# A four-layer graph-attention kernel: x ahead of the other loads at the start, its second part issued from ACT's queue, and a new set of due times

## The chip, the cores and the metric

The kernel runs on one core of one Trainium2 chip. The metric is the device time of one execution in microseconds (us); the median of six runs is given, and one further execution was taken with the hardware profiler. The core's engines each run their own instruction stream in order: TensorE (PE, with its weight loads as PEld), VectorE (DVE), ScalarE (ACT), GpSimd (POOL) and SyncE (SP), which issues most DMAs. They wait for one another by semaphores.

## The reference

x has 16 graphs of 1024 nodes and 256 features in float32; adj is one symmetric 1024 x 1024 adjacency matrix for all. Four attention layers follow each other. Each takes h = relu(layernorm(x)) and adds to x:

```
layer 0, 3:  Wh = h W (4 heads of 64); e_ij = leaky(s_i + t_j) per head, from two score vectors a
             softmax over j where adj_ij is set; out = elu(alpha Wh)
layer 1:     the same with one head of 256
layer 2:     e_ij = leaky((h W1)_i . (h W2)_j); out = relu(softmax(e) (h W3))
x = x + out
```

## The kernel before, in words

`tile_gnn_stack` runs `fast`, and a general version only where a check of the inputs fails; it does not run here. A "batch" is one graph, a unit of work is (batch, layer), and 64 of them are interleaved.

In layers 0, 1 and 3 the exponential of a leaky score is written as a maximum of products of per-node factors, so that no score matrix is computed: DVE makes a 128 x 512 tile p = max(row, ke) * mask in one instruction (`weigh`, line 1117 for the four-head layers 0 and 3, line 1208 for layer 1), and PE multiplies it with val (`attend`, into the accumulators acc, or accb for layers 1 and 2). A four-head unit has 64 such p tiles. A pool of 8 p buffers lies between DVE and PE. In layer 2 PE computes the scores (`score`), ACT takes exponentials (lines 1235 and 1236) and DVE finishes them (1240, 1241). `product` (line 579) issues every matmul of this kind as two of 64 columns, at line 582.

A unit begins with its prologue: `statistics` (lines 822, 823, on DVE, one pair for each 128 nodes), `norm`, `norm2`, `norm3` (rstd on DVE line 855, the power on POOL line 858, nshift on DVE line 861), h on ACT (line 891), a transposition of h, the projection by w on PE, and its eviction on ACT (lines 972, 975) and, in some units, DVE (line 983). The transposition goes through planes (ACT line 914), a DMA transpose issued by SP (line 918) and a copy (ACT line 932), but for the first unit (0, 0) and the last (15, 3), where `direct` is set: there PE transposes (lines 906, 929), the work is cut in parts of 2, 2 and 4 tiles (`PARTS`) or 4 and 4, and the factor rows come from PE (`spread`, lines 1025, 1029) and not over DRAM (lines 1051, 1064). A unit ends with reciprocal (1150), division (1161, 1164), elu (1083 to 1097; the sum with x on POOL at line 1097 where `filling` is set, else DVE line 1090) and, after layer 3, a store (1188).

The x tiles, one per batch, have five buffers; at the start four of them hold raw quarters of adj. `load_x` (line 628) loads a batch in parts. `weight` (line 645) loads a weight matrix and its score vectors, and puts their products into extra columns (line 684 the products, 697 or 701 the sums); for w0, loaded from ACT's queue, all of this runs on DVE, for the others the products are on POOL. `mask_steps` (line 721) loads the quarters of adj on SP (729), compares them on DVE (737), transposes on PE (595) and keeps them as bytes (750).

None of this is written in the order in which it runs. Each piece is added to a `Plan` (line 79) with an engine, an assumed cost, a due time, what it comes after, and what buffers it takes and gives. `Plan.order` (line 102) walks through assumed time: an idle engine takes, of the pieces that are ready and whose buffers are free, the one with the smallest due time. The resulting list is the order of the instructions. An "after" only shapes this list; the waits on the chip come from the data. The due times come from tables at the top (lines 49 to 73): START, LEAD, STEP, WHEN and EARLY for all units in periods of 190, LATER and AHEAD for single units of batches 0 to 3 and 12 to 15. So a changed cost or due time near the start can move work in all of the run.

Of the kernel before, what the change touches and what calls it, by code (L numbers as in the profile page):

```python
# [43 lines left out]
PARTS = (((0, 4), (4, 8)), ((0, 2), (2, 4), (4, 8)))  # L44

PERIOD, EARLY = 190.0, 0.7407
START = {0: 0.0, 1: 1.0372, 2: 2.297, 3: 3.5524}  # L50
LEAD = {0: 0.7046, 1: 0.4612, 2: 0.2956, 3: 1.6786}
STEP = {0: 0.01, 1: 0.0686, 2: 0.0892, 3: 0.0445}
WHEN = {
    (1, "weights"): ((-0.5242, 0.0026), (-0.1464, 0.0419)),
    (1, "attended"): ((0.7567, 0.0147), (0.2574, 0.106)),
    (2, "weights"): ((-0.0331, 0.0103), (0.3531, 0.0135)),
    (2, "attended"): ((0.642, 0.0926), (0.4636, 0.0079)),
}

LATER = {  # L60
    (1, 0): 0.596, (1, 1): 0.958, (13, 2): 0.03, (13, 3): 0.392, (14, 3): -0.089, (0, 2): -0.137, (12, 2): 0.2,
    (13, 1): -0.61, (13, 0): 0.042, (0, 1): 0.165, (14, 2): 0.012, (12, 3): 0.381, (15, 2): 0.061,
    (14, 1): 0.153, (0, 3): -0.204, (0, 0): 0.005, (15, 1): 0.169, (3, 0): -0.106, (3, 2): -0.226,
    (3, 1): -0.037, (3, 3): 0.253, (14, 0): -0.403, (15, 3): 0.422, (12, 0): 0.216, (2, 2): -0.002,
    (2, 3): -0.052, (12, 1): -0.053, (1, 3): 0.022,
}
AHEAD = {
    (1, 0): 0.818, (15, 3): 0.338, (12, 1): 1.914, (15, 1): 0.404, (1, 3): -1.162, (0, 3): 0.168,
    (14, 2): 0.163, (14, 1): -0.3, (1, 1): -0.058, (0, 2): 0.142, (13, 1): 0.271, (3, 1): 0.197, (14, 3): 0.426,
    (3, 3): -0.404, (2, 2): 1.115, (15, 0): -0.042, (12, 0): 0.12, (1, 2): 0.321, (2, 3): -0.168,  # L70
    (3, 2): -0.354, (2, 1): -0.221, (13, 3): -0.364, (0, 1): 0.057, (12, 3): 0.014, (0, 0): -0.016,
    (13, 2): -0.254,
}
# [466 lines left out]
def fast(  # L540
# [87 lines left out]
    def load_x(b, due, after=()):  # L628

        res = []  # L630
        for t0, t1 in PARTS[b == 0]:

            def fn(its=slice(t0, t1)):
                if its.start == 0:
                    x_tiles[b] = buf("x", [P, NT, F], name="xt")
                nc.sync.dma_start(
                    out=x_tiles[b][:, its, :], in_=x[b].rearrange("(t p) f -> p t f", p=P)[:, its, :]
                )

            s = plan.add(SP, 0.5, due, fn, after, take=() if t0 else ("x",))  # L640
            after = (s,)
            res += [landed(s, due, 128 * (t1 - t0))] * (t1 - t0)
        return res

    def weight(w, name, due, a=None, heads=0, own=1):
# [9 lines left out]

        s = landed(plan.add(engine, 0.5, due, load), due, 256)
        if a is None:
# [10 lines left out]

        s2 = landed(plan.add(engine, 0.5, due, load_a, take=("p1",)), due, own * d)

# [7 lines left out]
        for c in range(KC):  # L678

            def columns(c=c):  # L680
                wa = tiles["wa", c] = buf("u", [P, heads, 2, d], name="wa")
                for side in range(2):
                    of = tiles["a"][:, :, side, :]
                    (nc.vector if first else nc.gpsimd).tensor_mul(
                        wa[:, :, side, :],
                        t[:, c, :F].rearrange("p (h d) -> p h d", h=heads),
                        of if own == heads else of.to_broadcast([P, heads, d]),
                    )

            m = plan.add(*((DVE, 0.7) if first else (POOL, 2.0)), due + 0.5, columns, (s, s2, *done), take=("u",))  # L690
            done = []
            for hd in range(1 if first else heads):

                def add_up(c=c, hd=hd):
                    wa, to = tiles["wa", c], t[:, c, F:].rearrange("p (s h) -> p h s", s=2)
                    if first:
                        nc.vector.tensor_reduce(to, wa, AX.X, OP.add)
                        return
                    for side in range(2):
                        junk = small.tile([P, F], BF16, name="junk_a", bufs=1)[:, :d]  # L700
                        nc.scalar.activation(
                            junk, wa[:, hd, side, :], AF.Identity, accum_out=to[:, hd, side : side + 1]
                        )

                give = () if not first and hd < heads - 1 else ("u", "p1") if c == KC - 1 else ("u",)
                done.append(
                    plan.add(*((DVE, 0.6) if first else (ACT, 1.1)), due + 0.5, add_up, (m, *done[-1:]), give=give)
                )
        return t, done[-1]

    first_x = load_x(0, SOON)

# [3 lines left out]

    w0, w0_ready = weight(w_l0, "w0", SOON, a_l0, 4, 4)
    plan.add(ACT, 1.6, SOON, warm)
    plan.add(DVE, 0.2, SOON, lambda: nc.vector.tensor_copy(ident_b, ident))

    def mask_steps():
        done = {}
        for n, (half, jh) in enumerate(((0, 0), (0, 1), (1, 0), (1, 1))):
            due, quarter = 15.0 + n if half else SOON + n, {}

# [4 lines left out]

            loaded = landed(plan.add(SP, 0.9, due, load, take=("x",)), due, 1024)
            for t in range(HT):
# [5 lines left out]

                s = plan.add(DVE, 0.45, due, positive, (loaded,), take=("h",), give=("x",) if t == HT - 1 else ())

# [10 lines left out]

                s = plan.add(*((ACT, 0.6) if half else (DVE, 0.45)), due, keep, (s,), give=("pp",))
                done.setdefault((half, jh), []).append(s)
# [11 lines left out]
    def w12_steps(due):  # L765
        tiles, last = {}, []
        for k, w in enumerate((w1_l2, w2_l2)):
# [4 lines left out]

            loaded = landed(plan.add(SP, 0.5, due, load, take=("p1",)), due, 256)
            for cc in range(KC):
# [53 lines left out]
    class Layer:  # L828
# [7 lines left out]
        def prologue(self, due, step, stats, direct=False):  # L836
# [12 lines left out]
            for n, its in enumerate(slice(*part) for part in parts):  # L849
# [28 lines left out]

                at = due - (len(parts) - n - 1)
                s = plan.add(DVE, 0.2, at, norm, (*stats[its], ready[-1] if n else None))  # L880
                s = plan.add(POOL, 2.0, at, norm2, (s,))
                take = () if n else (tag,) if self.gat else (tag, "hq")
                ready += [plan.add(DVE, 0.2, at, norm3, (s,), take=take)] * (its.stop - its.start)
            copies, evicted = [], []
            for n, t0 in enumerate(range(0, NT, 2)):
# [37 lines left out]
                def kept(t0=t0):  # L923
                    if self.gat:
                        T["hT", t0] = buf("hTp", [P, KC, 2 * P])
                    else:
                        T["hT", t0] = self.hT[:, :, t0 * P : (t0 + 2) * P]
                    if direct:
                        nc.scalar.copy(T["hT", t0], T["tp", t0])
                        return  # L930
                    bits = T["hT", t0].bitcast(U16).rearrange("p c (q s) -> p c q s", s=2)
                    nc.scalar.copy(bits, T["tp", t0].rearrange("p s c q -> p c q s"))  # L932

                take = ("hTp",) if self.gat else ()
                if direct:
                    s = plan.add(PE, 0.47, at, turned, (s,), take=("pp",), give=("h", "h"), wide=True)
# [8 lines left out]
                for k in range(2):  # L945
# [40 lines left out]
                    cost = 0.32 if many or not self.gat else 0.65 if heads == 1 else 1.05  # L986
                    s2 = plan.add(ACT, cost, at, evict, (s2,), give=() if many else ("pp",))
                    if many:
                        s2 = plan.add(DVE, 0.43, at, scaled, (s2,), give=("pp",))
# [27 lines left out]
            if direct:  # L1017
                for half in range(2):
                    for hd in range(heads):
# [7 lines left out]
                        def keep(half=half, hd=hd):  # L1027
# [3 lines left out]
                        s = plan.add(  # L1031
                            PE, 0.44, at + (half * heads + hd) * 0.01, spread, tuple(evicted[half * HT : (half + 1) * HT]),
                            take=("pp", f"row{heads}"), wide=True,
                        )
                        self.row_ready[half, hd] = plan.add(ACT, 0.6, at, keep, (s,), give=("pp",))
                return
# [16 lines left out]

            s = plan.add(PE, 0.14, at, factors, tuple(evicted), take=("pp",))
            s = plan.add(ACT, 0.35, at, keep, (s,), give=("pp",))
# [336 lines left out]
    for start, b, layer in sorted(order):  # L1392
# [3 lines left out]
        if layer:  # L1396
            stats = lays[b, layer - 1].closed
        elif b:
            loads[b] = load_x(b, due - 0.45 * PERIOD, tuple(lays[b - 1, 0].ready))
            stats = [statistics(b, t, due, (loads[b][t],)) for t in range(NT)]  # L1400
        else:
            due, step = SOON, 0.1
            stats = [statistics(b, t, due - 2.5 + t // 2 * 0.9, (loads[b][t],)) for t in range(NT)]
        lay.prologue(due, step, stats, direct=(b, layer) in ((0, 0), (B - 1, 3)))
# [70 lines left out]
```

## Time and profile before

| | us |
|---|---|
| median of 6 runs (2978.39 to 2981.16) | 2978.75 |
| the profiled execution | 2977.96 |
| its span, first to last instruction | 2976.1 |
| PE busy | 2910.5 |
| DVE busy | 2646.0 |
| ACT busy | 1924.4 |
| POOL busy | 234.0 |
| start of the first matmul | 11.68 |
| start of the last group of attends | 2967.09 |

Busy is the time in which an engine had an instruction running; the rest of the span it was idle, and the profile names what ended each idle time (its releaser). Matmuls are pipelined, so their single durations overlap; what one costs in a row is read from the start-to-start distance. The granted clock is the share of its full speed at which PE was clocked; over the whole span it was 0.993.

### The profile page before, as it was taken

What the parts mean: (1) busy time and instruction counts of PE and PEld (TensorE: products, weight loads), DVE (VectorE), ACT (ScalarE), POOL (GpSimd) and SP (SyncE); (2) the same over time, 40 slices, a digit from 0 to 9 for tenths busy, and PEclk for the clock granted to TensorE, in tenths of its full rate; (3) what the DMA queues carried; (4) which work ended last, traced back from release to release, by engine and by line L of the source; (5) the groups of instructions that cost most, each with busy time, mean ns of one, the idle gap of its engine ahead of it and who ended that gap; (6) DMA issues with size and microseconds to landing.
All of it is one profiled execution on the core that took longest, in us unless ns stands there. A gap on an engine that the chain in (4) does not pass through costs nothing.

```text
span 2976.1 us, 108647 instructions
## 1 busy us (share of the span) xinstructions
PE 2910.5 (98%) x47954; PEld 2325.3 (78%) x47954; DVE 2646.0 (89%) x5286; ACT 1924.4 (65%) x4776; POOL 234.0 (8%) x151
## 2 busy tenths in 40 slices
PE   7899999999999999999999999999999999999997
PEld 5776868779697887978779787786877869796876
DVE  8989988899898899989899898988999999796698
ACT  6767776785655767566775656766656684656543
POOL 2111100000000000000000100000000010000001
PEclk9899999999999999999999999999999999999999
DMA  4422223333222333413232231331413332121210
GB/s 130 94 55 59 66 48 98 71 61 74 46 71 58 69 73 59 80 40 85 48 66 77 48 78 44 74 72 38 91 41 70 76 62 57 41 58 34 52 36 25
DMA packets 344048, 188.06 MB, mean 63 GB/s; under 512 B 268880, under 2 KB 304400, under 8 KB 343568
## 3 DMA queue, kind: packets, MB, share of 16 engines
q1 hardware_dynamic: 343152, 180.51, 27.2%
q8 instruction: 378, 6.19, 0.9%
q14 instruction: 102, 0.84, 0.1%
q10 hardware_dynamic: 416, 0.52, 0.1%
HBM read 98.63 MB, written 17.33 MB: 39 GB/s over the span
## 4 chain that ended last, share of the span: by engine, by line
PE 84%; DVE 13%; ACT 1%; issue 1%; DMA 0%; POOL 0%; SPq 0%; DVEq 0%; POOLq 0%
PE pp L582 31%; PE accb L582 27%; PE acc L582 26%; DVE p L1117 8%; DVE o L1088 1%; DVE bn L822 1%; DVE xt L1090 0%; DVE p L1241 0%; DVE mv L823 0%; DVE p L1240 0%; ACT hTp L932 0%; POOL xt L1097 0%; DMA xt<-in_x_dram 0%; DMA turned<-planes 0%; DVE rden L1150 0%
## 5 line engine op out<-in xcount | busy, mean ns | idle before, releaser
L1117 DVE SCALAR_TENSOR_TENSOR p<-row,ke,mask 128x512 f32<-128x512 f32 x2048 | 1460.3, 768 | 33.6 <-PE acc L582 32.3
L582 PEld LDWEIGHTS acc<-val,p 128*64 128x64 f32 x32768 | 1073.1, 139 | 121.1 <-issue 47.0
L582 PE MATMUL acc<-val,p 128*64 128x65 f32 x32768 | 1075.0, 223 | 39.1 <-DVE p L1117 34.0
L582 PE MATMUL accb<-val,p 128*64 128x257 f32 x8192 | 928.1, 380 | 0.0
L582 PEld LDWEIGHTS accb<-val,p 128*64 128x64 f32 x8192 | 736.1, 136 | 130.0 <-issue 4.1
L582 PE MATMUL pp<-qT,hT 128*64 128x512 f32 x2048 | 461.4, 592 | 0.0
L582 PE MATMUL pp<-w,hTp 128*64 128x264 f32 (+1 forms) x3072 | 380.0, 385 | 3.6 <-ACT hTp L932 2.1
L582 PEld LDWEIGHTS pp<-qT,hT 128*64 128x64 f32 x2048 | 171.2, 137 | 211.7 <-issue 209.1
L582 PEld LDWEIGHTS pp<-w,hTp 128*64 128x64 f32 x3072 | 244.4, 137 | 82.6 <-issue 11.4
L891 ACT ACTIVATE h<-xt,nshift,rstd 128x256 f32<-128x256 f32 x512 | 275.5, 596 | 37.9 <-DVE nshift L861 37.9
L1240 DVE SCALAR_TENSOR_TENSOR p<-u,p 128x512 f32<-128x512 f32 x256 | 175.8, 687 | 127.8 <-ACT p L1236 127.4
L1275 ACT ACTIVATE o<-accb,rdens 128x256 f32<-128x256 f32 x128 | 60.7, 474 | 347.7 <-DVE rdens L1267 341.4
L914 ACT COPY planes<-h 128x512 uint16<-128x512 uint16 x496 | 281.6, 620 | 0.0
L932 ACT COPY hTp<-turned 128x1024 uint16<-128x1024 uint16 x184 | 214.1, 1167 | 28.5 <-DMA turned<-planes 28.3
L822 DVE BATCH_NORM_STATS2 bn<-xt 128x6 f32<-128x256 f32 x512 | 211.9, 414 | 13.1 <-DMA xt<-in_x_dram 5.1
L1235 ACT ACTIVATE u<-pp 128x512 f32<-128x512 f32 x256 | 153.0, 598 | 104.4 <-PE pp L582 79.1
L1164 ACT ACTIVATE o<-acc,rden 128x64 f32<-128x64 f32 x572 | 132.6, 317 | 113.2 <-DVE rden L1150 99.7
L858 POOL TENSOR_TENSOR rstd<-rstd,neg_half 128x8 f32<-128x8 f32 (+2 forms) x67 | 124.6, 1860 | 976.2 <-DVE rstd L855 643.6
L1241 DVE TENSOR_TENSOR p<-p,mask 128x512 f32<-128x512 f32 x256 | 179.2, 700 | 8.8
L1097 POOL TENSOR_TENSOR xt<-xt,o 128x1024 f32<-128x1024 f32 x35 | 97.6, 2787 | 1131.2 <-DVE o L1088 1024.3
L1208 DVE SCALAR_TENSOR_TENSOR p<-row,ke,mask 128x512 f32<-128x512 f32 x256 | 180.2, 738 | 0.3 <-DMA row<-er_d 0.3
L977 ACT ACTIVATE val<-pp,val 128x64 f32<-128x64 f32 (+1 forms) x640 | 180.0, 348 | 0.0
(87 smaller groups left out, 1912.7 us busy)
## 6 DMA issues: line engine op xcount, KB each, us to landing
row<-er_d SPq DMA_DIRECT2D x272, 256.0 KB, 3.6
xt<-in_x_dram SPq DMA_DIRECT2D x31, 512.0 KB, 5.2
out_dram<-xt SPq DMA_DIRECT2D x31, 512.0 KB, 3.4
raw<-in_adj_dram SPq DMA_DIRECT2D x4, 1024.0 KB, 15.4
raw<-in_adj_dram SPq DMA_DIRECT2D x16, 256.0 KB, 3.5
turned<-planes SPq DMA_TRANSPOSE x248, 3.1
xt<-in_x_dram SPq DMA_DIRECT2D x2, 256.0 KB
w<-in_L_gnn_W_dram SPq DMA_DIRECT2D x2, 256.0 KB
```

The source lines that it names most:

```text
L582: nc.tensor.matmul(to[c : c + COLS], stationary[:, c : c + COLS], moving, start=start, stop=stop, skip_group_check=True,)
L822: nc.vector.bn_stats(st, x_tiles[b][:, t, :])
L891: nc.scalar.activation(h, x_tiles[b][:, t, :], AF.Relu, bias=T["shift"][:, t : t + 1], scale=T["rstd"][:, t : t + 1],)
L914: nc.scalar.copy(to[:, :, :, k, :], of)
L932: nc.scalar.copy(bits, T["tp", t0].rearrange("p s c q -> p c q s"))
L977: nc.scalar.mul(to[:, hd, :], of[:, hd, :], a[:, hd, :])
L1117: nc.vector.scalar_tensor_tensor(p, lay.rows[half, hd], lay.ke[:, lay.heads + hd, jt : jt + 1], mask_of(half, jt), op0=OP.max, op1=OP.mult)
L1164: nc.scalar.mul(to[:, t, :], acc[:, t, :d], rden[:, t, :])
L1208: nc.vector.scalar_tensor_tensor(p, lay.rows[half, 0], lay.ke[:, 1, jt : jt + 1], mask_of(half, jt), op0=OP.max, op1=OP.mult)
L1235: nc.scalar.activation(u, e, AF.Exp, scale=1.0 - SLOPE)
L1240: nc.vector.scalar_tensor_tensor(p, u, 1.0, p, op0=OP.max, op1=OP.mult)
L1241: nc.vector.tensor_mul(p, p, mask_of(half, jt))
```

## The change

The first load of x is cut as before into parts of 2, 2 and 4 tiles, but the second part is issued by ACT and no longer by SP, at the head of ACT's program; the table load and the warm-up exponential come next, and then the loads of w0 and its score vectors, which were ACT's first instructions before. In the plan, all other loads come after the first x or after the first quarter of the mask; on SP their order stays as it was but for one late pair of loads.

The statistics and norms of (0, 0) get earlier due times, ahead of masks and weights. Of the column products of w0, those of the second half of its rows go from DVE to POOL. In the two `direct` units the factor rows wait for the eviction on ACT (`factored`) and not for the scaling on DVE too, and the first half of them is due earlier. Several assumed costs are new (0.36 for a comparison, 0.65 for a mask copy, POOL's power by its size). All tables of due times have new values. `TURNED_ON_PE` names the same two units as `direct` did.

The diff, cut to these points:

```diff
-PERIOD, EARLY = 190.0, 0.7407
-START = {0: 0.0, 1: 1.0372, 2: 2.297, 3: 3.5524}
-LEAD = {0: 0.7046, 1: 0.4612, 2: 0.2956, 3: 1.6786}
+PERIOD, EARLY = 190.0, 0.8711
+START = {0: 0.0, 1: 1.0292, 2: 2.3297, 3: 3.7503}
+LEAD = {0: 0.5727, 1: 0.718, 2: 0.2478, 3: 2.1041}
...
 LATER = {
-    (1, 0): 0.596, (1, 1): 0.958, (13, 2): 0.03, (13, 3): 0.392, (14, 3): -0.089, (0, 2): -0.137, (12, 2): 0.2,
+    (1, 0): 0.176, (1, 1): 0.626, (13, 3): 0.356, (0, 2): -0.59, (12, 3): 0.485, (14, 1): 0.247, (0, 3): -0.2,
...
 AHEAD = {
-    (1, 0): 0.818, (15, 3): 0.338, (12, 1): 1.914, (15, 1): 0.404, (1, 3): -1.162, (0, 3): 0.168,
+    (1, 0): 1.089, (15, 1): 0.578, (1, 3): -0.801, (0, 3): 0.053, (14, 1): -0.086, (0, 2): 0.67, (13, 1): 0.384,
...
-                nc.sync.dma_start(
+                (nc.scalar if apart else nc.sync).dma_start(
                     out=x_tiles[b][:, its, :], in_=x[b].rearrange("(t p) f -> p t f", p=P)[:, its, :]
                 )
-            s = plan.add(SP, 0.5, due, fn, after, take=() if t0 else ("x",))
-            after = (s,)
+            s = plan.add(ACT if apart else SP, 0.5, due, fn, after, take=() if t0 else ("x",))
+            after = () if b == 0 else (s,)
...
-        s = landed(plan.add(engine, 0.5, due, load), due, 256)
+        begin = () if first else tuple(mask_ready[0, 0])
+        s = landed(plan.add(engine, 0.5, due, load, begin), due, 256)
...
-            def columns(c=c):
+            def columns(c=c, at_once=first and c == 0):
...
-                    (nc.vector if first else nc.gpsimd).tensor_mul(
+                    (nc.vector if at_once else nc.gpsimd).tensor_mul(
...
-    first_x = load_x(0, SOON)
+    first_x = load_x(0, SOON - 10.0)
...
-    w0, w0_ready = weight(w_l0, "w0", SOON, a_l0, 4, 4)
-    plan.add(ACT, 1.6, SOON, warm)
+    plan.add(ACT, 1.6, SOON - 9.0, warm)
+    w0, w0_ready = weight(w_l0, "w0", SOON - 6.0, a_l0, 4, 4)
...
-            due, quarter = 15.0 + n if half else SOON + n, {}
+            due, quarter = 15.0 + n if half else -1.5 if jh else SOON - 5.2, {}
...
-                at = due - (len(parts) - n - 1)
+                at = due - 5.0 * (len(parts) > 1)
...
                     s2 = plan.add(ACT, cost, at, evict, (s2,), give=() if many else ("pp",))
+                    factored.append(s2)
...
-                            PE, 0.44, at + (half * heads + hd) * 0.01, spread, tuple(evicted[half * HT : (half + 1) * HT]),
+                            PE, 0.44, at - 2.5 * step * (1 - half) + (half * heads + hd) * 0.01, spread, tuple(factored[half * HT : (half + 1) * HT]),
...
-            due, step = SOON, 0.1
-            stats = [statistics(b, t, due - 2.5 + t // 2 * 0.9, (loads[b][t],)) for t in range(NT)]
+            due, step = SOON - 5.0, 0.1
+            stats = [statistics(b, t, due - 2.5 + t // 2 * 0.5, (loads[b][t],)) for t in range(NT)]
```

## The prediction

> **What bounds the kernel now.** First the page: totals, then the chain that ended last.
>
> ```profile
> span 2976.1 us, 108647 instructions
> ...
> PE 2910.5 (98%) x47954; PEld 2325.3 (78%) x47954; DVE 2646.0 (89%) x5286; ACT 1924.4 (65%) x4776; POOL 234.0 (8%) x151
> ...
> PE 84%; DVE 13%; ACT 1%; issue 1%; DMA 0%; POOL 0%; SPq 0%; DVEq 0%; POOLq 0%
> ```
>
> PE is bound: 65.6 us of the span are PE idle. The busy times by stretch say where (columns: stretch, length, PE, PEld, DVE, ACT and POOL busy, granted PE clock, DMA share, GB/s).
>
> ```profile
> 0.00:10.00 10.00, 0.00 (x0) 0.00 (x0) 3.32 (x13) 1.49 (x2) 1.54 (x10) 1.00 0.82 254
> ...
> 80.00:100.00 20.00, 11.71 (x281) 10.93 (x279) 18.13 (x40) 8.95 (x40) 4.42 (x2) 0.76 0.14 42
> ...
> 300.00:2700.00 2400.00, 2391.02 (x39128) 1920.66 (x39126) 2160.92 (x4343) 1588.63 (x3873) 172.59 (x107) 1.00 0.29 64
> ...
> 2940.00:2976.10 36.10, 23.99 (x568) 20.65 (x562) 29.59 (x49) 10.35 (x28) 2.86 (x1) 0.91 0.11 33
> ```
>
> About 40 us idle lie before 300, 9 in the 2400 us of the middle, 16 after 2900. At both ends DVE is the busy engine and PE waits for its p tiles. The PE waits of 0 to 300 (what, for what: sum, times, longest):
>
> ```profile
> PE acc L582 <- DVE p L1117: 22.2, 16, 8.3
> PE pp L906 <- ACT h L891: 11.7, 1, 11.7
> ```
>
> Last the timeline of the opening (start, length, instruction, in brackets the idle time before).
>
> ```profile
> 4.38 0.43 DVE L822 BATCH_NORM_STATS2 bn<-xt 128x6 f32<-128x256 f32 x1 [2.80 <-DMA xt<-in_x_dram]
> ...
> 7.71 0.43 DVE L822 BATCH_NORM_STATS2 bn<-xt 128x6 f32<-128x256 f32 x1 [1.96 <-DMA xt<-in_x_dram]
> ...
> 9.25 0.43 DVE L822 BATCH_NORM_STATS2 bn<-xt 128x6 f32<-128x256 f32 x1 [0.37 <-DMA xt<-in_x_dram]
> ...
> 10.86 0.13 DVE L861 SCALAR_TENSOR_TENSOR nshift<-mv,rstd 128x2 f32<-128x2 f32 x1
> ...
> 25.17 3.70 POOL L684 TENSOR_TENSOR wa<-w,a_bc 128x256 f32<-128x256 f32 x4 [9.65 <-DVE a_bc L674]
> ...
> 26.11 3.31 DVE L1117 SCALAR_TENSOR_TENSOR p<-row,ke,mask 128x512 f32<-128x512 f32 x3
> ```
>
> DVE waits 1.96 and 0.37 us for the second and third part of x, and nshift (ready on POOL since 6.62) stands behind six statistics that need them; so the first h, and the first matmul at 11.68, are late. Everything here hangs on DVE.
>
> **The change, part by part.** I read the order of instructions on each engine in both builds. The work is the same but for two column products of w0, which go from DVE to POOL. I sum each engine's work in program order. DVE, start to start in a row in the first 300 us: weigh L1117 0.668 (7.35 for 11 at 77.35), statistics 0.53, pos 0.35, mask copy 0.61, val 0.33, elu tail L1088 1.11 wide and 0.36 narrow, column product 0.35. PE: an attend of one p tile 0.475 (16 x 0.0297), accb 0.109 a matmul, projection 0.11, score 0.215.
>
> *1. Opening.* x part 2 goes to ACT's queue at 0.75, beside part 1; w0 and a follow behind ACT's table load (1.28) and the warm-up, so at about 2.9 instead of 0.75. SP's other loads keep their order and are issued one x load earlier (1.47 / 3 = 0.49). nshift for tiles 0 and 1 now stands behind three statistics, not six, and the first two groups of transposes come ahead of the mask's. Gain for DVE: the 1.96 and 0.37, if part 2 lands like w0 did on that queue (issue to landing 4.0, so at 4.75, before DVE asks at 5.7). Against it: a is needed on DVE at about 9.3 (4.4 plus eight statistics and the small ones); issued 2 us later it may make DVE wait 0 to 2.0, I take 1.0. Everything behind DVE's a_bc, the w0 columns, the masks, then waits. The two products on POOL: in the row at 25.17 four of them stretched three weighs from 2.0 to 3.31, 0.33 each, so 0.65; bounds 0 and 2 x 0.93 (the whole POOL time). I take 0.4, as some of it falls beside mask work. Sum besides the 0.7 of moved DVE work: -2.33 + 1.0 + 0.4 = **-0.9**, bounds -2.3 and +1.5.
>
> [...]
>
> *2. What PE lacks in the opening.* For each weigh take DVE's sum up to its end, PE's sum ahead of its attend, and the difference: what PE must idle if DVE never waits. Real times of before add an extra (start, waits, POOL).
>
> | weigh | before: DVE, PE, difference; real end, extra | after: DVE, PE, difference |
> |---|---|---|
> | 61 | 70.8, 57.5, 13.3; 86.0, 15.2 | 70.1, 57.5, 12.6 |
> | 127 | 140.2, 131.1, 9.1; 162.5, 22.3 | 138.1, 110.2, 27.9 |
> | 144 | 167.8, 139.2, 28.6; 194.5, 26.7 | |
> | 157 | 176.7, 150.6, 26.0; 204.3, 27.7 | 176.2, 152.4, 23.9 |
>
> Before, the hole is 28.6 + 26.7 = 55.3 at weigh 144, where PE's last wait of the opening ends (194.61). After, the largest are 27.9 + 22.3 = 50.2 at 127 and 23.9 + 26.7 = 50.6 at 157 (the last 1.0 of its extra was DVE waiting for PE). With -0.9 that is 49.7: **-5.6**. The reason in words: before, (1,0)'s first weigh stands behind 12 statistics of batches 2 and (0,1), where PE idles 8.29; after, two stand there and others are spread, and (0,2)'s projection is reached with more PE work done. Bounds: -9 (the 3.5 us that DVE waited for PE between 85 and 130 go too), -1 (extras fall as in before, step 1 at its worst).
>
> Of the extras after weigh 61, 3.0 is one stretch of four weighs (5.70 at 69.53) beside a POOL add. [...]
>
> *3. Middle.* The dues (START, LEAD, WHEN, LATER, AHEAD) are new for all batches. PE is 99.6% busy there; the most that can be won is 9 us, and before's PE waits for p in it are 6.9. Of the layer chains (last attend to next projection, in PE work between) most have more room than before: layer 2 to 3 of batches 5 to 8 14.9, now 36.3; (0,1) to (0,2) 10.5, now 16.2. The 14.9 sufficed, as the waits there are at most 0.35. Tighter: (14,3) 15.2 to 14.3, (0,3) 18.2 to 15.1. And batch 14: its x takes the buffer of (9,3), and from there to its projection lie 35.8 us of PE work, 103.2 before; batch 15 43 instead of 96. I take 0, from -3 to +10.
>
> *4. End.* DVE can run 8 p tiles ahead (the pool). For each of the last 170 weighs: DVE work left from it, less PE work left after the attend 8 tiles earlier. Largest before: 58.2 - 45.4 = 12.8; after: 54.1 - 40.3 = 13.8. **+1.0**; bounds 0 and +3 (half clock behind longer waits; 0.91 in the last row).
>
> Sum: -5.6 + 0 + 1.0 = -4.6. The profiled execution took 2977.96 (span 2976.1), 0.8 under the median 2978.75; so 2973.4 or 2974.2. I say **2974**.
>
> **Rivals.**
> 1. Forecast, 2974 (2969 to 2979). For it: PE waits on DVE p alone, 22.2 us. Chance 0.40.
> 2. Extras grow as DVE's order gets denser, part 2 of x lands no sooner: only the 0.7 and little more is won, the end gives 1.0 back: 2978. For it: all x parts share DMA at 0.82 busy. Chance 0.25.
> 3. The half-speed stretches go as well (clock 0.76 from 80 to 100), DVE no longer waits for PE: -9 + 1 and 1 from the middle: 2970. Against it: PE stays only 57% fed between weighs 61 and 91 (14.3 of 24.9 us). Chance 0.15.
> 4. Slower: the reload of batch 14. Chain by rows: last attend to store to x load 13.3 (2136.3 to 2149.6), landing 5.2, statistics 4.2, rstd and nshift 2.4, h 1.1, planes 1.15, transpose 3.1, copy 1.17: 31.6. It decides from 35.8 on; SP, which issues store, load and transposes in order, has waited up to 17.9 us for one planes copy. With 14 us of such waiting it is 9.8 late, PE stands, and -4.6 turns to about +7: 2986 with what follows in batch 15. Chance 0.20.
>
> **Numbers.** The 0.2% (about 6 us) that a measurement of this kernel can tell from no change lies at 2972.8 and 2984.7. Faster: rival 3 and half of the forecast, 0.35. Slower: most of rival 4 and a bad middle, 0.19. Same: 0.46. Range 2965 to 2986: from beyond rival 3 to rival 4.
>
> **What would show it.** Right: the second bn at under 0.5 us of waiting; nshift near 7.5 and the first PE matmul near 8.3 (11.68 now); a wait of DVE for a_bc or w0 near 9.5; first weigh near 21.5 (26.11); no PE wait for p over 4 us in 80 to 100; PE without waits from about 180; PE idle before 300 near 34; after 2900 near 17. Wrong: PE waits over 1 us between 2150 and 2500, or a DVE busy 100% with PE as idle as before.

## The result and the profile after

The changed kernel takes **2971.58 us** (median of 18 runs, 2969.17 to 2974.38), the kernel before 2978.91 (38 runs, 2975.93 to 2981.16): ratio 0.9975, 95% interval 0.9969 to 0.9981, so 7.3 us less. The profiled execution of the changed kernel took 2974.32 and is one of its longest; that of before, 2977.96, lay 0.95 under its median. Between the two profiles there are therefore only 3.6 us, and they are what the views below can explain; the rest is spread between executions, to which the last section comes back.

The page after, totals and chain:

```profile
span 2972.5 us, 108633 instructions
...
PE 2918.5 (98%) x47954; PEld 2301.4 (77%) x47954; DVE 2644.9 (89%) x5284; ACT 1922.8 (65%) x4776; POOL 227.1 (8%) x153
...
PE 83%; DVE 11%; ACT 2%; DMA 1%; issue 1%; POOL 0%; DVEq 0%; POOLq 0%; ACTq 0%
```

PE is idle for 54.0 us, 11.6 less, but busy for 8.0 more with the same 47954 matmuls. Busy time is a poor measure here, as matmuls overlap (32768 attends of 223 ns in the mean fill 1074.8 us) and their ends are modelled; where the 8.0 come from is not shown. The busy times by stretch (PE, PEld, DVE, ACT, POOL, then the granted PE clock):

```profile
0.00:10.00 10.00, 1.18 (x4) 0.58 (x4) 5.41 (x25) 3.02 (x5) 2.63 (x12) 1.00 0.82 256
80.00:100.00 20.00, 15.61 (x370) 14.02 (x368) 19.86 (x35) 8.60 (x37) 2.79 (x1) 0.84 0.16 55
300.00:2700.00 2400.00, 2390.16 (x38896) 1881.33 (x38894) 2145.05 (x4308) 1592.68 (x3887) 168.45 (x107) 1.00 0.30 64
2940.00:2972.50 32.50, 20.45 (x475) 17.46 (x470) 26.03 (x43) 9.32 (x26) 2.86 (x1) 0.90 0.11 37
```

In 80 to 100 PE is busy for 15.61 us where it was 11.71, DVE for 19.86 of 20. The 2400 us of the middle are no better filled than before (2390.16 against 2391.02). PE's waits of 0 to 300 (sum, times, longest):

```profile
PE acc L584 <- DVE p L1128: 16.1, 15, 2.1
PE pp L916 <- ACT h L901: 9.5, 2, 8.3
```

The one wait of 8.3 us for p has become several of at most 2.1. The opening in the timeline (start, length, instruction, idle time before):

```profile
4.35 0.43 DVE L831 BATCH_NORM_STATS2 bn<-xt 128x6 f32<-128x256 f32 x1 [2.78 <-DMA xt<-in_x_dram]
...
5.64 0.42 DVE L831 BATCH_NORM_STATS2 bn<-xt 128x6 f32<-128x256 f32 x1
...
6.96 0.43 DVE L831 BATCH_NORM_STATS2 bn<-xt 128x6 f32<-128x256 f32 x1 [0.16 <-DMA xt<-in_x_dram]
...
7.52 0.13 DVE L870 SCALAR_TENSOR_TENSOR nshift<-mv,rstd 128x2 f32<-128x2 f32 x1
...
22.94 0.75 DVE L1128 SCALAR_TENSOR_TENSOR p<-row,ke,mask 128x512 f32<-128x512 f32 x1 [0.48 <-ACT row L1040]
```

The second part of x is there when DVE asks (5.64, no wait), the third 0.16 late. The first matmul starts at 8.34, the first weigh at 22.94 (11.68 and 26.11 before).

To compare kernels with different orders I use **PE's lag** at a weigh: the start in the trace of the first matmul that uses its p, less the sum of PE's work ahead of it in program order, by the same row costs as in the prediction. A stretch in which PE waits for nothing leaves it as it is (but for a slow drift of the sum), a wait or half clock raises it. The second part of the table belongs to the experiments.

| kernel (one profile each) | weigh 175, behind the opening | 230 | 270 | 1980, before the end | last | median us |
|---|---|---|---|---|---|---|
| before | 56.7 | 57.8 | 58.4 | 56.8 | 75.5 | 2978.91 |
| changed | 50.8 | 50.3 | 54.2 | 53.3 | 71.8 | 2971.58 |
| e1 opening edits, old tables | 56.9 | 56.3 | 59.9 | 61.2 | 80.3 | 2982.15 |
| e2 tables alone | 54.9 | 54.4 | 58.2 | 55.3 | 72.8 | 2976.69 |
| e5 queue alone | 56.8 | 58.0 | 58.6 | 57.2 | 76.0 | 2977.01 |
| e11 tables and queue | 51.2 | 50.8 | 53.2 | 49.3 | 66.3 | 2973.78 |
| e3 changed, part 2 by SP | 53.2 | 52.8 | 56.6 | 54.2 | 71.4 | 2973.29 |
| e4 changed, products on DVE | 51.8 | 51.4 | 55.2 | 52.0 | 69.9 | 2972.05 |
| e7 changed, norms not first | 50.7 | 50.3 | 54.1 | 51.9 | 69.2 | 2973.01 |
| e8 changed, old late entries | 49.3 | 48.8 | 52.6 | 51.1 | 69.1 | 2971.99 |
| e10 changed, (1,0) of before | 49.3 | 50.2 | 54.6 | 51.4 | 69.3 | 2972.46 |
| e12 changed, rows after scaling | 47.9 | 47.4 | 51.1 | 48.5 | 65.6 | 2968.98 |

Up to weigh 175 the order of e8 is that of the changed kernel, and their lags differ by 1.5: that much one profile can be off. Of the 1.5, 0.9 is there at the first weigh already (22.02 in e8, 22.94 in the changed kernel): in both profiles PE started at half clock, and came to full clock at 15.3 us in e8 and at 17.1 in the other (last section). Small differences between two profiles have to be read with that in mind.

The medians in the table are from several chips, on which the kernel before took between 2978.23 and 2979.13; the ratios below are each to its own chip.

### The profile page after: what moved, and what is told of

Its sections match the earlier page's. It is cut to its first block, busy times and chain, and to the rows that moved or that the text cites. A ratio compares the mean times of both kernels' runs of the same rounds, so it can differ in the third digit from the quotient of the medians.

```text
span 2972.5 us, 108633 instructions
## 1 busy us (share of the span) xinstructions
PE 2918.5 (98%) x47954; PEld 2301.4 (77%) x47954; DVE 2644.9 (89%) x5284; ACT 1922.8 (65%) x4776; POOL 227.1 (8%) x153
## 4 chain that ended last, share of the span: by engine, by line
PE 83%; DVE 11%; ACT 2%; DMA 1%; issue 1%; POOL 0%; DVEq 0%; POOLq 0%; ACTq 0%
PE pp L584 30%; PE acc L584 27%; PE accb L584 26%; DVE p L1128 7%; DVE o L1099 1%; DVE bn L831 1%; DMA turned<-planes 1%; DVE p L1252 1%; DVE p L1251 1%; ACT h L901 0%; ACT planes L924 0%; DVE mv L832 0%; DVE xt L1101 0%; ACT hTp L942 0%; DVE p L1219 0%
## 5 line engine op out<-in xcount | busy, mean ns | idle before, releaser
L584 PE MATMUL acc<-val,p 128*64 128x65 f32 x32768 | 1074.8, 223 | 29.6 <-DVE p L1128 27.9
L584 PEld LDWEIGHTS accb<-val,p 128*64 128x64 f32 x8192 | 703.7, 136 | 162.7 <-issue 5.1
L584 PEld LDWEIGHTS pp<-qT,hT 128*64 128x64 f32 x2048 | 177.9, 137 | 206.8 <-issue 201.5
L901 ACT ACTIVATE h<-xt,nshift,rstd 128x256 f32<-128x256 f32 x512 | 275.1, 597 | 56.7 <-DVE nshift L870 56.1
L1247 ACT ACTIVATE p<-pp,shift_col 128x512 f32<-128x512 f32 x256 | 176.0, 687 | 0.0
```

The lines of the kernel that those rows point to most:

```text
L584: nc.tensor.matmul(to[c : c + COLS], stationary[:, c : c + COLS], moving, start=start, stop=stop, skip_group_check=True,)
L901: nc.scalar.activation(h, x_tiles[b][:, t, :], AF.Relu, bias=T["shift"][:, t : t + 1], scale=T["rstd"][:, t : t + 1],)
L1247: nc.scalar.activation(p, e, AF.Exp, bias=shift_col, scale=SLOPE)
```

## The experiments

Theory A is the prediction's: the new tables fill PE's hole before 300, and the opening edits move only its first microseconds. Theory B: the earlier x and the norms first are the gain. The intervals of the ratios are 0.0009 to 0.0014 to either side, 2.7 us and more, so the small differences are read from the profiles, one of each kernel.

**e1 and e2: the two halves of the change.** e1 puts all tables of before, PERIOD to AHEAD, into the changed kernel; e2 puts the new tables into the kernel before, the reverse edit. e1's:

```diff
-PERIOD, EARLY = 190.0, 0.8711
-START = {0: 0.0, 1: 1.0292, 2: 2.3297, 3: 3.7503}
+PERIOD, EARLY = 190.0, 0.7407
+START = {0: 0.0, 1: 1.0372, 2: 2.297, 3: 3.5524}
...
```

> The changed kernel with every table of due times of the kernel before (PERIOD to AHEAD); the edits of the opening stay. Theory A (the tables fill PE's hole, the edits of the opening only move its first us): by the sums of DVE's and PE's work in program order the largest hole is 27.6 at weigh 142 against 28.6 before, with before's extra of 26.7 less about 1.3 for the earlier x, so 53.0 against 55.3, and the end is as before (12.8): 2.3 us less than before, about 2976.5. PE then waits 6 to 9 us for p near 100, as before. Theory B (x ahead and the norms first give the gain): most of the 7.3 us stays, 2971 to 2973, and the long wait of PE near 100 is gone.

> The kernel before with the tables of due times of the changed one and nothing else of it; x, w0 and the products as before. Theory A: the hole is 29.0 + 22.3 = 51.3 at weigh 118 or 26.3 + 27.7 = 54 at weigh 157, the end 1.1 longer (13.9): 1 to 3 us less than before, 2975.5 to 2978, and no single wait of PE for p over 3 us between 60 and 140. Theory B: no gain at all, 2978 to 2980, since the waits at the start are all there. If both this kernel and the one with the old tables gain under 3 us, the two parts work only together (the later end of a hole decides).

e1: 2982.15, ratio 1.0012 (1.0003 to 1.0021), slower than before. e2: 2976.69, 0.9992 (0.9983 to 1.0001). By the medians one half costs 3, the other gains 2, together they gain 7. Theory A has e2's time, but not e1's, and e2's profile has the long wait for p that it ruled out (4.70 us at 70.86); Theory B has neither time. In e1 the first weigh starts at 22.02, 4.1 earlier than before, yet at weigh 175 PE's lag is that of before, and the wait of 7.88 us for p near 97 is there. Its loss is behind the opening, in waits that before does not have (timeline of e1, then the granted clock behind the wait):

```profile
526.51 9.29 PE L585 MATMUL accb<-val,p 128*64 128x257 f32 x68 [2.14 <-DVE p L1253]
```

```profile
527.00:530.50 3.50, 3.50 (x20) 0.52 0.19 66
```

The tables of before fit the order that before's opening led to. A changed opening shifts what the plan does next, and with the old tables waits of 0.71, 0.63, 1.14 and 2.14 us come up between 340 and 527.

**e3: part 2 of x back on SP.**

```diff
-                (nc.scalar if apart else nc.sync).dma_start(
+                nc.sync.dma_start(
```

> The changed kernel with the second part of x issued by SP again, between the first and the third; the order of all other instructions is the same. Theory of step 1 (the queue of its own lets part 2 land with part 1): DVE waits 1.5 to 2.0 us before the third statistics again, nshift and the first matmul come that much later (10 instead of 8.3), and as DVE sets the hole up to weigh 157, the whole kernel takes 1.5 to 2 us more, 2973 to 2974. [...]

2973.29, 0.9983 (0.9974 to 0.9992). DVE's timeline:

```profile
4.83 0.42 DVE L831 BATCH_NORM_STATS2 bn<-xt 128x6 f32<-128x256 f32 x1
...
10.94 0.43 DVE L831 BATCH_NORM_STATS2 bn<-xt 128x6 f32<-128x256 f32 x1 [4.94 <-DMA xt<-in_x_dram]
```

The time is what the theory of step 1 said, but by another wait than it names: the second part is in time, the third is late by 4.94 us, and the first matmul comes at 12.31. The whole loses 1.7 by the medians, 2.4 by the lag at weigh 175. What the second queue does is seen in the DMA view of 2 to 6 us (queue, packets, MB, share; q10 is ACT's, q1 carries the rest), first before, then changed:

```profile
q1 hardware_dynamic: 567, 0.56, 49.4%
q10 hardware_dynamic: 396, 0.50, 44.6%
```

```profile
q1 hardware_dynamic: 777, 0.78, 60.2%
q10 hardware_dynamic: 537, 0.53, 39.7%
```

In these 4 us both queues move bytes, in both kernels. Before, ACT's 0.50 MB was w0 and a, and SP's queue, with all of x (1.05 MB), had moved 0.56. Now ACT's 0.53 begins with x part 2 (0.26), and SP's 0.78 is about what its two parts hold (0.79). By the packets in the trace (x's are those of 1024 bytes on SP's queue) SP's share of x was through at 8.8 us before, at 6.4 in the changed kernel, at 6.2 in e5 and at 10.6 in e3.

In e5, where the queue is the only edit, the first matmul comes 2.5 us earlier (9.23 against 11.68); by the rows of the prediction the issue of one x load takes 0.49. In the views above both the total is higher in the changed kernel (1.30 MB against 1.06 in these 4 us) and x is earlier in it; which of the two counts for more was not separated. In e3 the first matmul comes 4.0 us later, but not all of that is the queue: x is later there than before (10.6 against 8.8), with the same loads in the same order on SP's queue. Its last quarter moved from 5.6 us on, beside the packets of the mask; why so slowly stays open.

**e4: both second products on DVE again.**

```diff
-                    (nc.vector if at_once else nc.gpsimd).tensor_mul(
+                    (nc.vector if first else nc.gpsimd).tensor_mul(
```

> The changed kernel with the two column products of the second half of w0 on DVE again, at the same place in the plan's list; all else the same. Step 1 (two products are 0.7 of DVE work; on POOL they stretch DVE by 0.4): the first weigh comes 0.3 later, and the time with it, 2971.9. [...] Second rival (DVE is not what the first weigh waits for: it waits 0.47 us for ACT ahead of each val): no change at all of the first weigh, 22.9, within 0.2.

2972.05, 0.9977 (0.9968 to 0.9986). The first weigh comes at 23.57 instead of 22.94, and the lag at weigh 175 is 1.0 higher, but the products are not the reason: PE came to full clock at 18.3 us in this profile and at 17.1 in the changed kernel's, and the last of the 32 projections of (0,0), on which the vals hang, starts 0.63 later (20.17 against 19.54). On DVE itself the move is nearly even. It takes two products away, and one of the four comparisons (pos) that follow is stretched beside POOL. The four, in the changed kernel and in e4:

```profile
11.33 1.96 DVE L746 TENSOR_SCALAR pos<-raw 128x512 bf16<-128x512 int32 x4
```

```profile
11.92 1.43 DVE L746 TENSOR_SCALAR pos<-raw 128x512 bf16<-128x512 int32 x4
```

In the changed kernel the first of the four takes 0.96 us where the others take 0.42, while POOL's products run (10.59 to 12.00). So two products on POOL cost DVE 0.54, where the sum of the prediction had 0.4 and its upper bound 1.86 (2 x 0.93); the mask copy behind the four starts at 13.21 and 13.26. Of the expectations the second rival fits, as DVE then waits for ACT in both. A gain of the move is not shown.

**e5: the queue alone, in the kernel before.** w0's load is issued right behind x part 2 on ACT.

```diff
-                nc.sync.dma_start(
+                (nc.scalar if b == 0 and its.start == 2 else nc.sync).dma_start(
```

> The kernel before, with the second part of x issued by ACT as its first instruction (w0, a and the table load after it) and nothing else; the order on the compute engines is that of before. The third run said that with the part on SP the wait of DVE is for the third part, 4.94 us, not for the second. Theory Q (the third part of x lands when the bytes ahead of it on SP's queue are through; taking 256 KB away lets it land 2 to 4 us sooner): both x waits of DVE (1.96 and 0.37) go, nshift at about 9, first weigh 2 us earlier than 26.1. What that is worth in the whole: Theory A (with the tables of before the hole is set at weigh 144, where DVE has waited for PE in between): at most 1 us, 2978 to 2979. Theory B (what the start gains goes through to the end): 2 us, 2976.5 to 2977.

2977.01, 0.9992 (0.9983 to 1.0001). DVE's waits shrink to these:

```profile
6.79 0.43 DVE L829 BATCH_NORM_STATS2 bn<-xt 128x6 f32<-128x256 f32 x1 [0.16 <-DMA xt<-in_x_dram]
9.45 0.49 DVE L681 TENSOR_SCALAR a_bc<-a_bc 128x256 f32<-128x256 f32 x2 [0.29 <-DMA a_bc<-in_L_gnn_a_dram]
```

The first matmul moves from 11.68 to 9.23, the first weigh only from 26.11 to 25.44. Most of what is lost between is the clock of this execution: PE came to full clock at 20.9 us. e11 has the same order on the compute engines up to 34 us, full clock from 16.0, and its first weigh at 23.81. The projections of (0,0) behind w0, in e5 and in e11:

```profile
16.95 5.29 PE L582 MATMUL pp<-w,hTp 128*64 128x264 f32 x28 [1.02 <-DVE w L704]
```

```profile
16.70 3.34 PE L581 MATMUL pp<-w,hTp 128*64 128x264 f32 x28 [1.02 <-DVE w L703]
```

By weigh 144 PE's lag is 55.2 against 55.5, so by the profile the start is eaten, as Theory A said; but only 0.7 us of it was left to be eaten. The median is 1.6 below that of before on its chip, near Theory B's 2976.5 to 2977, and its interval includes no change. e5 does not decide between the two; e1, where 4.1 us of earlier start are gone by weigh 175, speaks for Theory A.

**e6 and e9: room for (4,0).** After the opening the largest wait of the changed kernel is 2.24 us at 375, for the hTp of (4,0), which may begin only when (3,0) frees its val buffer. e6 lets (4,0) and (0,3) take the buffer later; e9 only (4,0), and not before (0,3) has its projection.

```diff
-                take = () if n else (tag,) if self.gat else (tag, "hq")
+                take = () if n or (b, layer) in APART else (tag,) if self.gat else (tag, "hq")
...
+            if (b, layer) in APART:
+                room = (plan.add(ACT, 0.01, due, opened, (ready[0],), take=(tag,)),)
```

> The changed kernel, but units (4,0) and (0,3) may begin their prologue before their val buffer is free (the buffer is taken at the first eviction and not at nshift). In the changed kernel (4,0) begins at 359.06, when the last attend of (3,0) frees the buffer, and PE waits 2.24 us for its hTp at 374.93, then runs at half clock for 6.8 us: 2.2 + 3.4 less what other waits take. Theory M (this wait and the half clock behind it are lost time): 3 to 5.5 us less than the changed kernel, 2966 to 2968.5, no wait of PE over 1 us and no half clock between 300 and 2900. Rival (PE is short of work there and waits for DVE's p in its place): 2971 to 2972, the wait is only renamed.

> As the sixth run, but only (4,0) may begin its prologue before its val buffer is free, and not before (0,3) has its projection: in the sixth run (4,0) held the two hTp buffers that (0,3) then waited for (5.03 us at 365). Up to 308 us of PE work the order is that of the changed kernel, and (4,0)'s projection now stands 7 us of work behind the end of (3,0) with its hTp long ready. Theory M (the wait of 2.24 and the 6.8 us at half clock behind it are lost time): the lag at weigh 270 stays near 50 where it jumped to 54, 3 to 4 us less in the whole, 2967.5 to 2969, if the later units (new order up to about 700 us, tightest rooms 10.1 and 11.7 of PE work) do not wait. Rival (PE then waits for DVE's p): 2971 to 2972.

(The half clock lasted 3.4 us, not 6.8.) e6: 2994.82, 1.0055 (1.0041 to 1.0069); e9: 2976.74, 0.9993 (0.9984 to 1.0002). Neither gains. e6, then e9, in PE's timeline:

```profile
365.35 6.21 PE L585 MATMUL pp<-w,hTp 128*64 128x264 f32 x32 [5.03 <-ACT hTp L948]
```

```profile
365.02 2.00 PE L585 MATMUL pp<-w,hTp 128*64 128x264 f32 x16
...
376.89 2.00 PE L585 MATMUL pp<-w,hTp 128*64 128x264 f32 x16 [2.65 <-ACT hTp L948]
```

In e6 PE's waits for hTp between 300 and 700 add up to 10.5 us. In e9 half of (4,0)'s projections run early, and the other half waits as before: only two hTp buffers exist, so the third pair of tiles can be begun only when a buffer is used up. The val buffer was not the last limit. The new order then waits 1.79 at 507 and more later.

**e7: the norms not first.**

```diff
-                at = due - 5.0 * (len(parts) > 1)
+                at = due - (len(parts) - n - 1)
...
-            due, step = SOON - 5.0, 0.1
+            due, step = SOON, 0.1
```

> The changed kernel with the due times of the statistics and norms of (0,0) of before: a_bc, the products and the sum of w0 come ahead of the last three statistics and two nshift on DVE; from about the thirtieth instruction on the order is the same. Theory N (norms first is a good part of the gain): w0 is ready 2 us sooner but h of the last six tiles 2 us later, the first weigh moves 1 to 2 us later and the whole with it, 2972.5 to 2973.5. Rival S (from 17 on DVE waits 0.47 us ahead of each of six vals, 3.0 in all, for ACT: there is room on DVE, the order ahead of it does not matter): first weigh within 0.5 us of 22.94, the time within 0.5 us of 2971.6.

2973.01, 0.9981 (0.9972 to 0.9990); first weigh 22.85, lag at weigh 175 50.7 against 50.8. By the profile the order of these instructions makes no difference (Rival S); the median lies where Theory N had it (2972.5 to 2973.5), and the 1.4 between the medians is within what the intervals allow. What the order is worth stays open within that.

**e8: the old late entries.** LATER and AHEAD of batches 12 to 15 as before.

```diff
-    (13, 3): 0.356,
+    (13, 3): 0.392,
...
```

> The changed kernel with the entries of LATER and AHEAD for batches 12 to 15 of before. The order is the same up to about 2100 us. By the sums the end is 13.7 against 13.8 and batch 14's x buffer has its old room. Theory A (all of the gain lies before 300): no difference, 2970.5 to 2972.5. Rival (the late entries give a part, or the tighter reload of batch 14 costs): 2 us or more in either direction, with PE waits over 1 us between 2100 and 2900 in the one of the two that is slower.

2971.99, 0.9977 (0.9968 to 0.9986): no difference. The late entries neither gain nor cost, and batch 14's tighter reload does no harm: PE's longest wait in 2150 to 2500 of the changed kernel is 0.85 us.

**e10: (1,0) of before.**

```diff
-    (1, 0): 0.176,
+    (1, 0): 0.596,
...
-    (1, 0): 1.089,
+    (1, 0): 0.818,
```

> The changed kernel with the entries of LATER and AHEAD for (1,0) of before (0.596 and 0.818 for 0.176 and 1.089), nothing else. By the sums the largest DVE hole falls from 28.3 at weigh 118 and 24.4 at 151 to 22.4 at 71 and 22.2 at 131, 20.6 between, and under 5 from 151 on; but from the last attend of (0,0) to the projection of (0,1) lie only 5.2 us of PE work instead of 12.9, for a chain of about 14. Theory H (the largest hole alone decides what PE loses before 300, and a wait inside it is free): hole 22.2 + 22 to 25 of extra = 44 to 47 against 51: 4 to 7 us less than the changed kernel, 2965 to 2968. Rival (the chain's 9 us of waiting come on top, with half clock behind them): 2972 to 2980, with a PE wait for hTp of 5 to 9 us near 85.

2972.46, 0.9978 (0.9969 to 0.9987). The hole by the sums was 6 us smaller, the measured lag at weigh 175 is 49.3, as in e8: nothing gained. PE waits 2.80 for the late chain at 92.75 and then 9.81 for p at 102.91. The extra of this order is not that of the other: at weigh 127 the lag is 48.0, where the sums and the old extra of 22 to 25 gave 44 to 47. Theory H holds only as far as the extra can be carried over. The time is in the rival's range, though the wait for the chain is 2.80 and not 5 to 9.

**e11: e2 and e5 together.**

> The kernel before with the tables of the changed one and x's second part on ACT's queue as ACT's first instruction: the second and the fifth run together. If the two add up: 1.6 us less than the tables alone, 2975.1, and 3.5 more than the whole change, which is then what the order of the opening (norms first, factor rows first, products on POOL) is worth. Theory T (with the new tables DVE never waits for PE before weigh 118, so all of the earlier x goes through; in the fifth run it was eaten by weigh 144): as much as the first weigh comes earlier, 0.7 to 2.5 us, 2974 to 2976, the lag at weigh 144 53 to 54.7 against 55.4. Rival (the first weigh does not hang on x but on the pace of w0's products and the vals): 2976.5 to 2977, the lag as with the tables alone.

2973.78, 0.9984 (0.9975 to 0.9993). Its edit is those of e2 and e5. The first weigh moves from e2's 26.32 to 23.81 and the lag at weigh 175 falls from 54.9 to 51.2: **with the new tables the earlier x goes through**, 2.5 us by the first weigh and 3.7 by the lag. In both profiles full clock came before the projections of (0,0) could run in a row (17.5 and 16.0). Theory T is right; the time is just below its 2974 to 2976. That the old tables let nothing through is shown by e1 and not by e5 beside e11: by the medians the queue is worth 1.6 us in e5 and 2.9 here, which their intervals do not tell apart.

**e12: factor rows after the scaling.**

```diff
-                            PE, 0.44, at - 2.5 * step * (1 - half) + (half * heads + hd) * 0.01, spread, tuple(factored[half * HT : (half + 1) * HT]),
+                            PE, 0.44, at + (half * heads + hd) * 0.01, spread, tuple(evicted[half * HT : (half + 1) * HT]),
```

> The changed kernel with the factor rows of the direct units waiting for the scaling on DVE again and with their old due times: all eight projections of (0,0) stand ahead of the first factor rows on PE, and four masks more behind them. Theory F (this edit is what brings the first weigh forward, by 2 to 3 us, since DVE needs only four vals for it): first weigh at 25 to 26 instead of 22.9, the whole 2 to 3 us later, 2973.5 to 2974.5. Rival (the sums of DVE's work up to weigh 118 are the same, 131.2 to 130.6; what DVE does not weigh early it spends on masks that it has to do anyway): the time within 0.7 us of 2971.6, the lag at weigh 118 49 to 50.5.

2968.98 (2968.15 to 2970.27, 7 runs), 0.9971 (0.9960 to 0.9982). First weigh 23.32, not 25 to 26, so Theory F is wrong; the lag at weigh 118 is 47.8 and the time 2.6 below 2971.6, so the rival's figures are missed too. No gain of this part of the change is seen. Without it the kernel is the fastest of all here: its seven runs all lie under the changed kernel's median, but on a chip where before took 2978.23, and the intervals of the two ratios overlap. The edit does a little more than its text says: in the units that are not direct the factors (line 1065) wait for the scaling again as well, where DVE scales; that, too, is a part of the change. Behind 300 us the order on DVE differs in two places up to 2850. Why it is faster was not tried further.

## Why the prediction was right, point by point

The prediction said 2974; the time is 2971.6, inside the forecast's own 2969 to 2979, but at its lower end and beyond the 0.2% (2972.8) on the faster side, which had 0.35 and not the most. The sum was −4.6, the medians differ by 7.3 and the two profiles by 3.6: it lies between.

*1. Opening, DVE: −0.9.* Right for x, wrong in two other terms. The x waits of 1.96 and 0.37 became 0 and 0.16; nshift came at 7.52 and the first matmul at 8.34 (7.5 and 8.3 predicted). The mis-sized term is the wait for a, +1.0: it was 0. w0 and a were held to be issued at about 2.9, behind the table load. The rows of ACT and its queue show that they are not:

```profile
0.75 0.48 ACTq L640 DMA_DIRECT2D xt<-in_x_dram  x1
...
1.26 1.28 ACT L723 ACT_TABLE_LOAD   x1 [1.26 <-PEq L1467]
...
1.48 0.37 ACTq L658 DMA_DIRECT2D w<-in_L_gnn_W_dram  x1
...
1.89 0.48 ACTq L669 DMA_DIRECT2D a_bc<-in_L_gnn_a_dram  x1
```

Both are issued while the load (1.26 to 2.54) runs. The products' +0.4 measured 0.54 (e4). A term that the sum did not have: DVE waits 0.47 us for ACT ahead of each of the next vals, 3.0 in all (1.3 before), and the first weigh came at 22.94, not 21.5. Half clock has a part in these waits: in e8, with the same order and full clock 1.8 us sooner, they are 2.2 and the first weigh is at 22.02. The step can be read at weigh 61. Its extra was 15.2 before, is 85.3 less 70.1, 15.2, in the changed kernel, and 14.3 in e8: 0 in the one profile and −0.9 in the other, which is the predicted total from terms that missed in both directions.

*2. The hole: −5.6.* Right: weigh 157 ended at 201.7 with 152.4 of PE work ahead, 49.3, where 49.7 was predicted. By the lag at weigh 175 it is −5.9. The place was given too late: the lag is set by weigh 118 (50.2), and from 143 us on no wait of PE before 300 is over 0.41 (at 188.53; the prediction said none from about 180). The shares are wrong, and that the total came out is in part luck: the prediction gave 4.7 to the order behind the opening and 0.9 to the opening. By the lag at weigh 175 the tables alone take 1.8 (e2) and the earlier x on top of them 3.7 (e11), together 5.5, each give or take the 1.5 that one profile can be off. With the old order a DVE that starts earlier stands waiting for PE: for PE's releases of p buffers and sums it waits 6.7 us between 24 and 200 in e1 where it waited 3.6 before, and 2.5 in the changed kernel. So the earlier start of e1 is given back by the old order; the changed kernel, with the same opening, keeps it.

*3. The middle: 0.* Mis-sized, within its bounds. Between weighs 230 and 1980 the lag rises by 3.0 where it fell by 1.0 before (in e4, with the same order there, it rises by 0.6): 1.6 to 4.0 to the bad. Most of it comes by weigh 270, at the wait for (4,0) and the 3.4 us at half clock behind it (3.9, where before has 0.6). The prediction weighed the rooms of (14,3), (0,3) and of batch 14's reload, and all of these held; it did not look at the room between the last attend of one four-head unit and the projection of the next but one, which takes over its val buffer.

*4. The end: +1.0.* Wrong sign, small: 18.5 against 18.7 in the lag.

By weigh 230 the changed kernel is 7.5 ahead, 1.6 more than at 175, mostly since before waits once more for p there, which the changed kernel does not:

```profile
249.16 1.26 PE L582 MATMUL acc<-val,p 128*64 128x65 f32 x32 [1.00 <-DVE p L1117]
```

The terms −7.5, +3.3 (to weigh 270), +0.7 (to 1980) and −0.2 (the end) add up to the −3.7 between the two profiles. The further 3.7 between the medians lie in which execution was profiled. Rival 2 (nothing but 0.7 won) is refuted by the lag. Rival 3 (half speed goes too) came true in part: the stretch of before at 191 to 198 is gone, but one at 375 is new. Rival 4 did not occur; of its +7, 9.8 less 4.6 is 5.2, and the rest had no working. Three readings were off without weight in the sum: the 6.9 us of waits for p are those of 300 to 2900, and 6.3 up to 2700; between rstd at 5.58 and nshift at 10.86 stand five statistics, not six, and the stretch of four weighs at 69.53 lies beside a POOL add and two POOL products, not the add alone. Of the signs, PE's idle time before 300 was 29.0 (34 predicted), after 2900 it was 15.1 (17).

Left open: why the last quarter of x moved so slowly in e3; why e12 is faster; and what of the 2.2 us between the medians of e11 and the changed kernel comes from which of the remaining edits.

## What to carry to other kernels

An edit at the start and the schedule behind it are not separate: the opening edits made the kernel 3.1 us slower with the old tables and 5.1 us faster with the new ones. Find out whether the engine that is sped up stands waiting further on before counting a gain through to the end. Removing a buffer's wait pays only if the next buffer of the same chain (here two hTp behind the val) has room. Before a difference of a microsecond between two profiles is given to an edit, compare the clock of the two: what e4 and e5 show at the first weigh looks like an effect of the edits, and is for the most part the time at which PE came to full clock.

## What the runs showed of the hardware

**PE started at half clock, for a time that varied from profile to profile.** The clock's record begins with an entry of full clock. Where projections of (0,0) run ahead of it, their matmuls follow each other at 0.43 us a pair (the changed kernel from 15.73 to 17.05; also e4, e5, e7, e9, e10, e12); behind it at 0.22 (the changed kernel from 17.31, before from 19.50). (The views print a granted clock of 1.00 for the time ahead of the entry, as in 0 to 10 above.) It came at 15.1 us in e1, 15.3 in e8, 16.0 in e11, 17.0 in before, 17.1 in the changed kernel, 18.3 in e4 and 20.9 in e5.

**In the profiles of before and of the changed kernel the half-clock stretches lie on steps of 3.413 us.** By the clock records of the two traces they start at 75.0, 92.1, 191.1, 2928.6 and 2952.5 in before, which are 5, 29, 802 and 7 steps of 3.413 us apart, and at 78.6, 95.6, 136.6, 375.5, 2921.9 and 2949.2 in the changed kernel, 5, 12, 70, 746 and 8 steps apart. They last one to four steps each (3.41 to 13.65 us); one more in each, at 2973.0 and 2969.6, is cut by the end. So a wait does not always cost the same. The same wait for (4,0) and the 32 projections behind it, in the changed kernel and in e11:

```profile
374.93 5.47 PE L584 MATMUL pp<-w,hTp 128*64 128x264 f32 x32 [2.24 <-ACT hTp L942]
```

```profile
375.35 4.11 PE L581 MATMUL pp<-w,hTp 128*64 128x264 f32 x32 [2.24 <-ACT hTp L938]
```

With a granted clock of 0.50 in 375.5 to 378.9 the group takes 5.47 us, with 1.00 throughout in e11 4.11. In the changed kernel the wait lies in one step (372.1 to 375.5, PE idle for 2.24 of 3.41 us), in e11, if its steps are counted on from its full clock at 16.0, across two (1.28 and 0.96). In the two traces, from the first full clock to PE's last attends, the steps sort by PE's idle time as I counted it from the matmuls' records: every step at full clock with up to 1.43 us idle was followed by full clock, every one with 1.62 or more by half clock (five in before, six in the changed kernel); half clock went on behind steps with 0.86 us idle or more and ended behind steps with 0.28 or less. What sets these figures is not shown. A wait of 2.24 us was followed by half clock in the changed kernel's profile and not in e11's. e11's profiled execution has one half-clock stretch after 2900 where the changed kernel's has three (granted clock 0.96 and 0.92 over 2900 to 2967), and at 2969.18 is the shortest of its eleven (to 2974.7).
